# Attention and graph convolution on one core: where the last two items' GpSimd additions stand, and who turns the last pair of heads

## The chip, the cores and the metric

The kernel runs on one core of a Trainium2 chip. The metric is the device time of one execution in microseconds (us). The engines are TensorE (PE in the profile, with PEld for its weight loads), VectorE (DVE), ScalarE (ACT), GpSimd (POOL) and the queues that issue DMA transfers (SP and ACT). Each engine works through its own instructions in program order[...].

## What is computed

There are 32 items; each is a 512x512 matrix `x`, and all share one adjacency matrix. Two layers follow each other, each with a residual and a layer norm:

```python
# layer 0: attention with 8 heads of 64, masked by adj
q, k, v = x @ Wq + bq, x @ Wk + bk, x @ Wv + bv
weights = softmax(q k^T / sqrt(64) + where(adj == 0, -1e9, 0))
x = layernorm(x + weights v)
# layer 1: graph convolution
norm_adj = adj * deg**-0.5 (rows) * deg**-0.5 (columns)
x = layernorm(x + norm_adj @ (x @ weight) + bias)
```

All inputs and outputs are 32-bit floats.

## The kernel before

A 512x512 matrix lies in SBUF as four row blocks of 128 partitions. The heads are handled in pairs `g`, in the order `ORDER = (0, 2, 1, 3)`, so there are 4 pairs for each of the 32 items and `S = 128` steps `k` in one long loop. A step forms the transposed scores of its pair in two halves (`scores`: TensorE into the PSUM tile `sc`, VectorE into the tile `e` with the mask, ScalarE the exponential in place), multiplies the previous pair's `e` with its values (`values`, PSUM tile `av`, heads on the partitions, rows along the free axis), and adds the `e` tiles up on GpSimd (`accumulate`), for the softmax sums that TensorE then forms (`sums`).

The projections use a seven-product scheme on 256-wide halves, and so does the convolution's second product (`second`, seven pieces `s[0]` to `s[6]`). Each piece writes one of three PSUM buffers `mm` and is then added to the outputs by VectorE, or copied aside by ScalarE and added by GpSimd (`extend`) in item 30, whose convolution has `aside` set.

After the pairs of an item comes its finish: `inverse` (TensorE turns the sums, VectorE takes the reciprocal), `add` or, in the last item, `add_pair` (values times reciprocal plus residual, per block of 128 rows and pair), `measure` (mean and variance), `root` (GpSimd raises to the power -0.5), `norm` (the normalized block into `yT`, or `wv` in the last item, and a rounded copy `hi` scaled by the degree), `split` (the rest `lo`, so that hi and lo together keep the precision, and then GpSimd adds the layer's bias row `b1_r` to the block). The convolution's first product (`first`, or `block` in the last item) multiplies hi and lo of each block with the adjacency. `grow` scales the residual, `combine` forms the sums that the seven products need.

The work of one item is laid between the steps of the next by lists of pieces that are written out by hand, and the order in the lists is the order on each engine: a wrapper pins every instruction to program order. This is why nearly all rows of the profile have line L44, the wrapper's; rows are told apart by their tile names. The `shares` lists of the last item's branch (lines 783 to 791) say what runs behind the steps S-3, S-2 and S-1; lines 821 to 849 are the tail after the last step, where there is no further pair to hide work behind.

Names used below: `split(i)` makes `lo` of row block i; `s` is the list `second` of item 30's convolution, `h` and `held` that of item 29; `last` and `end` are the finish of item 31; `pairs[2]` and `pairs[3]` are the `add_pair` of the third and fourth pair in order; `early` and `late` are the two halves of `inverse`; `judge` counts how many sums lie in a safe range; `norm[i]` of odd i runs on VectorE in the last item.

The values of a pair must be turned from heads on partitions to rows on partitions. In `values`, VectorE transposes 32x32 blocks of `av` into the tile `yb`, and four DMA transfers put the blocks where they belong in `YT`; for the last pair two of the four are issued by ScalarE's queue.

Of the kernel before, what the change touches and what calls it, by code (L numbers as in the profile page):

```python
# [9 lines left out]
F32 = mybir.dt.float32  # L10
# [7 lines left out]
P = 128  # L18
H = 8
HD = 64  # L20
# [29 lines left out]
def unshifted(  # L50
# [323 lines left out]
    def values(s):  # L374

        b, g, jj = s
        e = E.pop(s)
        if jj == 0:
            AV[b, g] = ps_av.tile([P, N], F32, name="av")
        av = AV[b, g]  # L380
        for l in range(2):
            j = 2 * jj + l
            for k in range(2):
                tensor.matmul(
                    av[k * HD : (k + 1) * HD, :], V[b][:, j, ts(2 * g + k, HD)], e[l][:, k, :],
                    start=j == 0, stop=j == NT - 1,
                )
        if jj == 0:
            return

        yb = work.tile([P, 4, NT, 32], F32, name="yb", bufs=1)
        vector.transpose(
            yb.rearrange("p l i s -> p i l s"), av.rearrange("p (i r l) -> p i l r", i=NT, l=4)
        )
        if g == ORDER[0]:
            if b < B - 1:
                YT[b] = acts.tile([P, NT, D], F32, name="yT")
            else:  # L400
                YT[b] = wv[:, :NT].rearrange("p k u o -> p k (u o)")
        for q in range(4):
            queue = scalar if q > 1 and (b, g) == blocks[-1] else nc.sync
            queue.dma_start(
                YT[b][:, :, (4 * g + q) * 32 : (4 * g + q + 1) * 32],
                yb[32 * q : 32 * (q + 1)],
            )
# [42 lines left out]
    def finish(b):  # L450


        t = {}

        def inverse(cs):
            sT = SM[b]
            p = ps_mm.tile([P, NT, 2, 2, 32], F32, name="mm")
            for i in range(NT):
                tensor.transpose(p[:, i].rearrange("p a k r -> p (a k r)"), sT[:, ts(i, P)], ident)
            if cs[0] == 0:  # L460
                t["inv"] = small.tile([P, NT, H], F32, name="inv")
# [12 lines left out]
        def add(i):  # L474
            y = YT[b][:, i, :]
            vector.tensor_mul(
                y.rearrange("p (h d) -> p h d", h=H), y.rearrange("p (h d) -> p h d", h=H),
                t["inv"][:, i, :, None].to_broadcast([P, H, HD]),
            )
            gpsimd.tensor_add(y, y, R[b][i])  # L480

        def add_pair(i, g):

            y, r = YT[b][:, i, :], R[b][i]
            for h in (2 * g, 2 * g + 1):
                at = slice(h * HD, (h + 1) * HD)
                vector.scalar_tensor_tensor(
                    y[:, at], y[:, at], t["inv"][:, i, h : h + 1], r[:, at], op0=ALU.mult, op1=ALU.add
                )

        def measure(i):
            if i == 0:
                t["mv"] = small.tile([P, NT, 2], F32, name="mv")
            statistics(YT[b][:, i, :], t["mv"][:, i, :])

        def root(i=0, k=NT):
            rstd, add = roots(t["mv"][:, i : i + k], None)
            for n in range(k):
                t["rstd", i + n], t["add", i + n] = rstd[:, n : n + 1], add[:, n : n + 1]

        def norm(i):
            if i == 0:
                if b < B - 1:
                    HI[b], LO[b] = (acts.tile([P, NT, D], F32R, name=k, bufs=1) for k in ("hi", "lo"))
                    LO[b] = [LO[b][:, k, :] for k in range(NT)]
                else:
                    HI[b] = acts.tile([P, NT, D], F32R, name="hi2", tag="v")
                    lo = [acts.tile([P, 2, D], F32R, name="lo2", tag="kq", bufs=5) for _ in range(2)]
                    LO[b] = [lo[k // 2][:, k % 2, :] for k in range(NT)]
            x1 = YT[b][:, i, :]  # L510
            rstd, add = t["rstd", i], t["add", i]
            if b == B - 1 and i % 2:
                vector.tensor_scalar(x1, x1, rstd, add, op0=ALU.mult, op1=ALU.add)
            else:
                scalar.activation(x1, x1, AF.Identity, bias=add, scale=rstd)

            scalar.activation(HI[b][:, i, :], x1, AF.Copy, scale=dis[:, i : i + 1])

        def split(i):
            x1 = YT[b][:, i, :]  # L520
            vector.scalar_tensor_tensor(
                LO[b][i], x1, dis[:, i : i + 1], HI[b][:, i, :], op0=ALU.mult, op1=ALU.subtract
            )
            gpsimd.tensor_add(x1, x1, b1_r)

        def grow(i):
            x1 = YT[b][:, i, :]
            scalar.activation(x1, x1, AF.Copy, scale=rdeg[:, i : i + 1])

        def block(f):  # L530
            return [(0, f, (i,)) for i in range(NT)]

        return dict(
            early=[(0.6, inverse, ((0,),))], late=[(0.6, inverse, ((1,),))],
            pairs=[[(0, add_pair, (i, g)) for i in range(NT)] for g in ORDER],
            halves=[(0, root, (0, 2)), (0, root, (2, 2))],
            inverse=[(0.6, inverse, ((0, 1),))], add=block(add), measure=block(measure), root=[(0, root, ())],
            judge=[(0, judge, ())], norm=block(norm), split=block(split), grow=block(grow),
        )

    def weave(side, main):
# [8 lines left out]
    def convolve(b):  # L550
# [43 lines left out]
        def second(k, i, j):  # L594
# [15 lines left out]
                vector.tensor_add(of(y, 0, 0), of(y, 0, 0), p)  # L610
            elif k == 2:
                vector.tensor_add(t["e1"], t["e1"], p)
                if not aside:
                    extend(2)
            elif k == 3:
                t["u2"] = work.tile([P, 2, HALF], F32, name="u2", bufs=1)
                vector.tensor_add(t["u2"], t["e1"], p)
                if not aside:
                    extend(3)
            elif aside:  # L620
                t[k, "p"] = work.tile([P, 2, HALF], F32, name="side", tag="e", bufs=6)
                scalar.copy(t[k, "p"], p)
# [42 lines left out]
        def store(n, at):  # L665
# [18 lines left out]
            extend=[(0, extend, (k,)) for k in range(2, 7)],  # L684
# [8 lines left out]
    def run(pieces):  # L693
        for _, f, args in pieces:
            f(*args)
# [40 lines left out]
    run(weave(masks, keys_and_queries(0, 1)))  # L736
    one, two = turns(1)
    run(one)
    shares, rest = [], []
    for k in range(S + 1):  # L740
        b, at = divmod(k, G)
        if at == 1:
# [38 lines left out]
                    shares = cut(side, (8, 8, 8, 4))  # L781
            else:
                f, c, last = last, convolve(b - 1), finish(b)
                s, first, norm, split, pairs = c["second"], c["first"], f["norm"], f["split"], last["pairs"]
                shares = [
                    h[3:4] + f["measure"] + f["root"] + h[6:] + norm + f["judge"],
                    h[4:6] + split + last["early"] + first[:2] + held["measure"][:2] + first[2:3]
                    + held["measure"][2:] + first[3:] + c["parts"] + f["grow"],
                    held["root"] + s[:2] + pairs[0] + pairs[1],
                    [],  # L790
                ]
# [8 lines left out]
        if k:  # L800
# [3 lines left out]
            values((*blocks[k - 1], 1))  # L804
            if k % 2 == 0 and k < S:
                sums(blocks[k - 1][0], (k - 1) % G // 2)
        if k < S:
            accumulate((*blocks[k], 0))
            scores((*blocks[k], 1))
            if b == B - 1:  # L810
# [8 lines left out]
            run(shares.pop(0))  # L819

    end, e = last, convolve(B - 1)
    norm, split, block, pairs, extend = end["norm"], end["split"], e["block"], end["pairs"], c["extend"]
    run(end["late"] + s[2:3] + pairs[2] + held["store"] + s[3:4])
    run(sum((pairs[3][i : i + 1] + end["measure"][i : i + 1] for i in (0, 1)), []) + end["halves"][:1] + s[4:5])
    run(sum((pairs[3][i : i + 1] + end["measure"][i : i + 1] for i in (2, 3)), []) + end["halves"][1:] + s[5:6])
    run(norm[:2] + split[:1] + block[:1] + extend[:2] + norm[2:3])
    run(split[1:2] + block[1:2] + extend[2:4] + norm[3:] + split[2:3] + block[2:3] + split[3:] + block[3:] + end["judge"])

# [302 lines left out]
```

## Time and profile before

| what | value |
|---|---|
| time, median of 3 runs | 2931.66 us (2931.45 to 2931.84) |
| profiled span | 2929.5 us |
| granted TensorE clock, mean | 0.995 |
| TensorE busy | 2874.0 us, 98% |
| VectorE busy | 2081.8 us, 71% |
| GpSimd busy | 1813.3 us, 62% |
| ScalarE busy | 1059.1 us, 36% |
| `lo` in items 0 to 30 | 124 instructions, mean 1269 ns, shortest 735 ns |
| GpSimd's bias addition to a block of `yT` | 124 instructions, mean 1391 ns |
| GpSimd's addition of two `e` tiles | 126 instructions, mean 2356 ns |

A row of a timeline gives the start and the length in us, the engine, the operation, the output and inputs, shapes, how many instructions are merged, and in brackets the idle time of the engine just before and what ended it. Times count from the start of the span. In the page's group list, a busy time and a mean are given for each kind of instruction. A busy engine may still be waiting inside an instruction, so the mean of one and the same operation can differ from place to place; the shortest case tells what it takes by itself.

### The profile page before, as it was taken

The numbers are of one execution on the slowest core, as the hardware profiler recorded it, in microseconds if no ns is written. First come the engines' busy times: TensorE is split into PE (matmuls) and PEld (weight loads), VectorE is DVE, ScalarE is ACT, GpSimd is POOL, SyncE is SP. The second block draws the span as 40 slices with busy tenths as digits, with TensorE's granted clock in tenths as the row PEclk, the third lists the DMA queues.
The fourth block names the chain that finished last, engine by engine and source line by source line (L and its number), as shares of the span: only waits on it lengthen the run. The fifth ranks groups of instructions, "written<-read, shape, count | busy, mean of one in ns | idle before, by whom it ended". The sixth has DMA issues, their size and how long they took to land.

```text
span 2929.5 us, 35536 instructions
## 1 busy us (share of the span) xinstructions
PE 2874.0 (98%) x12966; PEld 1885.9 (64%) x12966; DVE 2081.8 (71%) x2926; ACT 1059.1 (36%) x1343; POOL 1813.3 (62%) x1139
## 2 busy tenths in 40 slices
PE   7999999999999999999999999999999999999997
PEld 5666666666666666666666666666666666666655
DVE  6677766677666777666776667776677766677677
ACT  1233333343333433333433334333333333343343
POOL 2566666656666666666666666666666666656665
PEclk9999999999999999999999999999999999999998
DMA  5111122112221121211122211122211122112211
GB/s 130 33 26 47 47 58 51 38 39 51 54 54 41 39 51 47 57 41 40 47 50 55 55 40 36 49 53 54 44 40 47 47 58 54 40 35 49 54 36 52
DMA packets 383401, 142.42 MB, mean 49 GB/s; under 512 B 280049, under 2 KB 349681, under 8 KB 383217
## 3 DMA queue, kind: packets, MB, share of 16 engines
q1 hardware_dynamic: 380720, 138.35, 19.8%
q10 hardware_dynamic: 2496, 1.70, 0.3%
q8 instruction: 104, 1.70, 0.2%
q14 instruction: 81, 0.66, 0.1%
HBM read 72.88 MB, written 33.55 MB: 36 GB/s over the span
## 4 chain that ended last, share of the span: by engine, by line
PE 74%; DVE 16%; ACT 6%; issue 2%; POOL 1%; DMA 0%; SPq 0%; DVEq 0%; POOLq 0%
PE mm L44 47%; PE sc L44 15%; PE av L44 12%; DVE u L44 3%; ACT yT L44 3%; DVE e L44 3%; DVE st L44 3%; ACT hi L44 2%; DVE lo L44 2%; DVE low L44 2%; POOL rstd L44 1%; ACT e L44 1%; DVE mv L44 1%; DVE kq L44 1%; DVE v L44 1%
## 5 line engine op out<-in xcount | busy, mean ns | idle before, releaser
L44 ACT ACTIVATE e<-e 128x1024 f32<-128x1024 f32 x512 | 540.6, 1057 | 1095.1 <-DVE e L44 1076.3
L44 DVE SCALAR_TENSOR_TENSOR e<-sc,maskT 128x1024 f32<-128x1024 f32 x512 | 600.3, 1213 | 83.1 <-PE sc L44 82.7
L44 POOL TENSOR_TENSOR acc<-acc,e 128x1024 f32<-128x1024 f32 x248 | 597.4, 2409 | 64.2 <-ACT e L44 54.4
L44 POOL TENSOR_TENSOR acc<-e 128x1024 f32<-128x1024 f32 x126 | 296.9, 2356 | 382.5 <-ACT e L44 271.4
L44 PE MATMUL sc<-kq 64*128 64x512 f32 x2048 | 518.9, 620 | 14.5 <-DVE e L44 14.5
L44 PE MATMUL mm<-xT,wk 128*128 128x256 f32 x1792 | 469.8, 385 | 1.0 <-DVE off L44 1.0
L44 PE MATMUL av<-e,v 128*64 128x512 f32 x2048 | 467.9, 599 | 0.0
L44 PE MATMUL mm<-xT,wq 128*128 128x256 f32 x1792 | 459.9, 379 | 0.0
L44 PE MATMUL mm<-wv,xT 128*128 128x256 f32 x1792 | 407.2, 385 | 18.2 <-DVE xT L44 11.7
L44 PEld LDWEIGHTS mm<-xT,wk 128*128 128x128 f32 x1792 | 332.7, 190 | 113.4 <-issue 69.7
L44 PEld LDWEIGHTS mm<-wv,xT 128*128 128x128 f32 x1792 | 338.3, 192 | 93.2 <-issue 24.3
L44 PEld LDWEIGHTS mm<-xT,wq 128*128 128x128 f32 x1792 | 340.9, 190 | 45.6
L44 PEld LDWEIGHTS sc<-kq 64*128 64x128 f32 x2048 | 174.2, 186 | 297.9 <-issue 171.9
L44 PEld LDWEIGHTS av<-e,v 128*64 128x64 f32 x2048 | 135.5, 136 | 316.2 <-issue 315.4
L44 DVE TENSOR_TENSOR kq<-u,mm 128x512 f32<-128x512 f32 x128 | 88.0, 688 | 238.0 <-PE mm L44 237.9
L44 POOL TENSOR_TENSOR yT<-yT,xr 128x512 f32<-128x512 f32 x124 | 193.6, 1590 | 80.5 <-DVE yT L44 80.5
L44 POOL TENSOR_TENSOR rstd<-ve,minus_half 128x4 f32<-128x4 f32 (+1 forms) x66 | 66.2, 1003 | 259.3 <-DVE nmu L44 259.3
L44 PE MATMUL mm<-w,zT 128*128 128x256 f32 x992 | 224.6, 379 | 0.0
L44 POOL TENSOR_TENSOR yT<-yT,b_r 128x512 f32<-128x512 f32 x124 | 171.2, 1391 | 56.4 <-DVE lo L44 56.4
L44 PEld LDWEIGHTS mm<-w,zT 128*128 128x128 f32 x992 | 188.4, 190 | 26.8 <-issue 1.5
L44 PE MATMUL mm<-adjT,hi 128*128 128x512 f32 x496 | 203.7, 411 | 0.0
L44 PE MATMUL mm<-adjT,lo 128*128 128x512 f32 x496 | 198.3, 400 | 5.2 <-DVE lo L44 5.2
(124 smaller groups left out, 3178.6 us busy)
## 6 DMA issues: line engine op xcount, KB each, us to landing
x<-in_x_dram SPq DMA_DIRECT2D x256, 128.0 KB, 2.9
out_dram<-y SPq DMA_DIRECT2D x127, 256.0 KB, 2.1
xr<-in_x_dram SPq DMA_DIRECT2D x124, 256.0 KB, 3.5
yT<-yb SPq DMA_DIRECT2D x496, 64.0 KB, 2.5
wv<-in_L_gnn_Wv_dram ACTq DMA_DIRECT2D x8, 128.0 KB, 4.5
wk<-in_L_gnn_Wk_dram SPq DMA_DIRECT2D x8, 128.0 KB, 4.3
wq<-in_L_gnn_Wq_dram SPq DMA_DIRECT2D x8, 128.0 KB, 4.5
yT<-in_adj_dram SPq DMA_DIRECT2D x1, 1024.0 KB, 6.6
```

Source lines behind the costliest of these rows:

```text
L44: return self.tc.keep_in_program_order(op(*args, **kwargs))
```

## The change

It has two aims. The first is that the last pair's values shall not go through VectorE's block transpose and a DMA: they are copied from PSUM to SBUF by ScalarE and VectorE, half each, TensorE transposes them into a PSUM buffer, and `add_pair` reads the values there. The second is the order on GpSimd in the last two items: its additions are put behind the VectorE operations that they keep from running. `split` becomes two parts, `low` (VectorE) and `lift` (GpSimd). In item 30 one `low` is put ahead of the last-but-one pair's second scores, two more between two pieces of `second`, the fourth behind them, then the four lifts, and only then the two additions of that pair's `e` tiles, which were issued with the scores before. In the tail, `extend(2)` and `extend(3)` go directly behind their products, `extend(4)` ahead of the second root, `extend(5)` behind the first lift, and the lifts behind the `lo` of the next blocks; `s[5]` goes ahead of the first `norm`.

```diff
@@ values @@
+        if (b, g) == blocks[-1]:
+            turned = work.tile([P, N], F32, name="avT", tag="yb", bufs=1)
+            scalar.copy(turned[:, :HALF], av[:, :HALF])
+            vector.tensor_copy(turned[:, HALF:], av[:, HALF:])
+            AV[b, g] = turned
+            return
...
-            queue = scalar if q > 1 and (b, g) == blocks[-1] else nc.sync
-            queue.dma_start(
+            nc.sync.dma_start(
@@ finish @@
+        def turn_values(g):
+
+            t["y"] = ps_mm.tile([P, NT, P], F32, name="mm")
+            for i in range(NT):
+                tensor.transpose(t["y"][:, i], AV[b, g][:, ts(i, P)], ident)
...
+                values = t["y"][:, i, ts(k, HD)] if (b, g) == blocks[-1] else y[:, at]
                 vector.scalar_tensor_tensor(
-                    y[:, at], y[:, at], t["inv"][:, i, h : h + 1], r[:, at], op0=ALU.mult, op1=ALU.add
+                    y[:, at], values, t["inv"][:, i, h : h + 1], r[:, at], op0=ALU.mult, op1=ALU.add
...
         def split(i):
-            x1 = YT[b][:, i, :]
-            vector.scalar_tensor_tensor(
-                LO[b][i], x1, dis[:, i : i + 1], HI[b][:, i, :], op0=ALU.mult, op1=ALU.subtract
-            )
-            gpsimd.tensor_add(x1, x1, b1_r)
+            low(i)
+            lift(i)
@@ second @@
                 vector.tensor_add(t["e1"], t["e1"], p)
-                if not aside:
-                    extend(2)
+                extend(2)
...
                 vector.tensor_add(t["u2"], t["e1"], p)
-                if not aside:
-                    extend(3)
+                extend(3)
@@ the last item's lists @@
+                within = low[:1]
                 shares = [
...
-                    h[4:6] + split + last["early"] + first[:2] + held["measure"][:2] + first[2:3]
-                    + held["measure"][2:] + first[3:] + c["parts"] + f["grow"],
+                    h[4:5] + low[1:3] + h[5:6] + low[3:] + lift + put_off + put_off + last["early"] + first[:2]
+                    + held["measure"][:2] + first[2:3] + held["measure"][2:] + first[3:] + c["parts"] + f["grow"],
@@ the step loop @@
-        if k < S:
+        if k == S - 2:
+            run(within)
+            scores((*blocks[k], 1))
+            pending += [((*blocks[k], jj),) for jj in range(2)]
+        elif k < S:
@@ the tail @@
-    run(end["late"] + s[2:3] + pairs[2] + held["store"] + s[3:4])
-    run(sum((pairs[3][i : i + 1] + end["measure"][i : i + 1] for i in (0, 1)), []) + end["halves"][:1] + s[4:5])
-    run(sum((pairs[3][i : i + 1] + end["measure"][i : i + 1] for i in (2, 3)), []) + end["halves"][1:] + s[5:6])
-    run(norm[:2] + split[:1] + block[:1] + extend[:2] + norm[2:3])
-    run(split[1:2] + block[1:2] + extend[2:4] + norm[3:] + split[2:3] + block[2:3] + split[3:] + block[3:] + end["judge"])
+    run(end["late"][:1] + pairs[2] + end["late"][1:] + s[2:3] + held["store"])
+    run(sum((pairs[3][i : i + 1] + end["measure"][i : i + 1] for i in (0, 1)), []) + end["halves"][:1] + s[3:5])
+    run(sum((pairs[3][i : i + 1] + end["measure"][i : i + 1] for i in (2, 3)), []) + extend[:1] + end["halves"][1:])
+    run(s[5:6] + norm[:2] + low[:1] + block[:1] + low[1:2] + block[1:2] + lift[:1] + extend[1:2] + norm[2:] + low[2:3])
+    run(block[2:3] + low[3:] + lift[1:2] + block[3:] + lift[2:] + end["judge"])
...
-    run(e["unload"] + e["parts"] + s[6:] + end["grow"] + extend[4:] + c["measure"][:2])
+    run(e["unload"] + e["parts"] + s[6:] + end["grow"] + extend[2:] + c["measure"][:2])
```

`late` now holds two entries: the reciprocal of the second half of the sums, and `turn_values` of the last pair. `extend` of item 30 now holds only `extend(4)` to `extend(6)`.

More of the change, by code (lines that the diff above doesn't have):

```diff
@@ L480, in add @@
             gpsimd.tensor_add(y, y, R[b][i])
+        def turn_values(g):
+            t["y"] = ps_mm.tile([P, NT, P], F32, name="mm")
+            for i in range(NT):
+                tensor.transpose(t["y"][:, i], AV[b, g][:, ts(i, P)], ident)
         def add_pair(i, g):
             y, r = YT[b][:, i, :], R[b][i]
-            for h in (2 * g, 2 * g + 1):
+            for k in range(2):
+                h = 2 * g + k
                 at = slice(h * HD, (h + 1) * HD)
+                values = t["y"][:, i, ts(k, HD)] if (b, g) == blocks[-1] else y[:, at]
                 vector.scalar_tensor_tensor(
-                    y[:, at], y[:, at], t["inv"][:, i, h : h + 1], r[:, at], op0=ALU.mult, op1=ALU.add
+                    y[:, at], values, t["inv"][:, i, h : h + 1], r[:, at], op0=ALU.mult, op1=ALU.add
                 )
@@ L517, in norm, with low, lift @@
             scalar.activation(HI[b][:, i, :], x1, AF.Copy, scale=dis[:, i : i + 1])
-        def split(i):
-            x1 = YT[b][:, i, :]
-            vector.scalar_tensor_tensor(
-                LO[b][i], x1, dis[:, i : i + 1], HI[b][:, i, :], op0=ALU.mult, op1=ALU.subtract
-            )
-            gpsimd.tensor_add(x1, x1, b1_r)
+        def low(i):
+            vector.scalar_tensor_tensor(
+                LO[b][i], YT[b][:, i, :], dis[:, i : i + 1], HI[b][:, i, :], op0=ALU.mult, op1=ALU.subtract
+            )
+        def lift(i):
+            gpsimd.tensor_add(YT[b][:, i, :], YT[b][:, i, :], b1_r)
+        def split(i):
+            low(i)
+            lift(i)
         def grow(i):
@@ L533, in finish @@
         return dict(
-            early=[(0.6, inverse, ((0,),))], late=[(0.6, inverse, ((1,),))],
+            early=[(0.6, inverse, ((0,),))], late=[(0.6, inverse, ((1,),)), (0.6, turn_values, (ORDER[-1],))],
             pairs=[[(0, add_pair, (i, g)) for i in range(NT)] for g in ORDER],
@@ L537, in finish @@
             inverse=[(0.6, inverse, ((0, 1),))], add=block(add), measure=block(measure), root=[(0, root, ())],
-            judge=[(0, judge, ())], norm=block(norm), split=block(split), grow=block(grow),
+            judge=[(0, judge, ())], norm=block(norm), split=block(split), low=block(low), lift=block(lift), grow=block(grow),
         )
@@ L683, in convolve @@
             second=[(2.1, second, (k, *args)) for k, args in enumerate(order)],
-            extend=[(0, extend, (k,)) for k in range(2, 7)],
+            extend=[(0, extend, (k,)) for k in range(4, 7)],
             halves=[[(0, measure_half, (n, i)) for n in range(2)] for i in range(2)],
@@ L738, in unshifted @@
     run(one)
-    shares, rest = [], []
+    shares, rest, within = [], [], []
     for k in range(S + 1):
@@ L783, in unshifted @@
                 f, c, last = last, convolve(b - 1), finish(b)
-                s, first, norm, split, pairs = c["second"], c["first"], f["norm"], f["split"], last["pairs"]
+                s, first, low, lift, pairs = c["second"], c["first"], f["low"], f["lift"], last["pairs"]
+                within = low[:1]
                 shares = [
-                    h[3:4] + f["measure"] + f["root"] + h[6:] + norm + f["judge"],
-                    h[4:6] + split + last["early"] + first[:2] + held["measure"][:2] + first[2:3]
-                    + held["measure"][2:] + first[3:] + c["parts"] + f["grow"],
+                    h[3:4] + f["measure"] + f["root"] + h[6:] + f["norm"] + f["judge"],
+                    h[4:5] + low[1:3] + h[5:6] + low[3:] + lift + put_off + put_off + last["early"] + first[:2]
+                    + held["measure"][:2] + first[2:3] + held["measure"][2:] + first[3:] + c["parts"] + f["grow"],
                     held["root"] + s[:2] + pairs[0] + pairs[1],
@@ L821, in unshifted @@
     end, e = last, convolve(B - 1)
-    norm, split, block, pairs, extend = end["norm"], end["split"], e["block"], end["pairs"], c["extend"]
-    run(end["late"] + s[2:3] + pairs[2] + held["store"] + s[3:4])
-    run(sum((pairs[3][i : i + 1] + end["measure"][i : i + 1] for i in (0, 1)), []) + end["halves"][:1] + s[4:5])
-    run(sum((pairs[3][i : i + 1] + end["measure"][i : i + 1] for i in (2, 3)), []) + end["halves"][1:] + s[5:6])
-    run(norm[:2] + split[:1] + block[:1] + extend[:2] + norm[2:3])
-    run(split[1:2] + block[1:2] + extend[2:4] + norm[3:] + split[2:3] + block[2:3] + split[3:] + block[3:] + end["judge"])
+    norm, low, lift, block, pairs, extend = end["norm"], end["low"], end["lift"], e["block"], end["pairs"], c["extend"]
+    run(end["late"][:1] + pairs[2] + end["late"][1:] + s[2:3] + held["store"])
[3 more added lines that the diff above has]
+    run(block[2:3] + low[3:] + lift[1:2] + block[3:] + lift[2:] + end["judge"])
     count = small.tile([P, 1], F32, name="count")
```

## The prediction

> **What bounds the kernel now.** I read the page's shares first. TensorE is busy for 98% of the span, so over 30 of the 32 items an edit on VectorE or GpSimd is worth nothing unless TensorE waits for it. The change touches only the last two items, so I then looked at their last 95 us by stretches (columns: stretch, length, busy time and instructions of PE, PEld, DVE, ACT and POOL, the granted clock, DMA share, GB/s).
>
> ```profile
> PE 2874.0 (98%) x12966; PEld 1885.9 (64%) x12966; DVE 2081.8 (71%) x2926; ACT 1059.1 (36%) x1343; POOL 1813.3 (62%) x1139
> 2834.00:2847.00 13.00, 13.00 (x66) 5.98 (x65) 11.21 (x21) 7.25 (x10) 5.50 (x5) 1.00 0.14 20
> 2847.00:2857.00 10.00, 4.84 (x14) 2.30 (x13) 9.70 (x7) 2.35 (x3) 9.47 (x5) 0.68 0.01 2
> 2857.00:2865.00 8.00, 8.00 (x27) 6.03 (x28) 2.75 (x8) 2.06 (x4) 2.38 (x3) 0.76 0.00 0
> 2865.00:2881.00 16.00, 16.00 (x80) 6.55 (x76) 11.02 (x26) 7.22 (x10) 10.54 (x8) 1.00 0.12 17
> 2892.00:2904.00 12.00, 11.20 (x42) 8.84 (x42) 11.63 (x18) 5.21 (x9) 11.37 (x9) 0.87 0.00 0
> 2904.00:2918.00 14.00, 12.72 (x56) 10.02 (x56) 13.08 (x27) 2.79 (x6) 13.32 (x12) 1.00 0.01 2
> ```
>
> TensorE loses half of the stretch from 2847 to 2857, where VectorE and GpSimd both look full; in the next one it is full but at a clock of 0.76. From 2892 on it is again VectorE and GpSimd that are full together. The timeline of the first hole says why:
>
> ```profile
> 2847.53 2.36 POOL L44 TENSOR_TENSOR wq<-e 128x1024 f32<-128x1024 f32 x1 [7.95 <-ACT e L44]
> 2847.91 8.66 DVE L44 SCALAR_TENSOR_TENSOR lo<-yT,dis,hi 128x512 fp32r<-128x512 f32 x4
> 2849.85 2.81 POOL L44 TENSOR_TENSOR wk<-e 128x1024 f32<-128x1024 f32 x1
> 2850.49 0.66 PE L44 MATMUL mm<-adjT,lo 128*128 128x512 f32 x1 [2.56 <-DVE lo L44]
> 2852.61 6.34 POOL L44 TENSOR_TENSOR yT<-yT,b_r 128x512 f32<-128x512 f32 x4
> 2853.25 0.80 PE L44 MATMUL mm<-adjT,lo 128*128 128x512 f32 x1 [1.67 <-DVE lo L44]
> ```
>
> Four lo subtractions take 8.66 us here, 2.17 each. The operation's own length is that of its shortest case, 735 ns among 124. Each lo waits for one GpSimd addition, and each addition for one lo: they alternate. TensorE waits for every lo. In the chain of waits that ended last the same stretch stands as VectorE's, then nearly everything from 2883.7 to 2907.5 with it:
>
> ```profile
> 2847.99 8.59 DVE lo L44 x4
> 2882.13 1.70 ACTq L44 DMA_DIRECT2D wv<-yb  x2
> 2886.46 0.47 DVE L44 SCALAR_TENSOR_TENSOR wv<-wv,inv,wk 128x64 f32<-128x64 f32 x2
> 2895.73 3.47 DVE L44 SCALAR_TENSOR_TENSOR lo<-wv,dis,hi 128x512 fp32r<-128x512 f32 x2
> 2899.13 1.27 DVE L44 TENSOR_SCALAR low<-inv 128x32 f32<-128x32 f32 x1
> 2900.43 1.22 DVE L44 SCALAR_TENSOR_TENSOR low<-inv,low 128x32 f32<-128x32 f32 x1
> 2904.00 0.68 DVE L44 COPY xT<-sc 128x512 f32<-128x512 f32 x1
> ```
>
> The first line is the chain's, the rest the timeline's. The turned values of the last pair are sent at 2882.1 and first used at 2886.46. The tiny check of the sums (128x32) takes 1.27 and 1.22 us, and TensorE's output waits for it until 2904.0.
>
> **What the Trainium skill says.** "SBUF — State Buffer", section Who interferes with whom: VectorE and GpSimd share a port pair as an exclusive lock; a VectorE instruction with two SBUF inputs, or a copy or tensor_scalar in a two-port mode, and a GpSimd instruction reading SBUF exclude each other for their whole length; a VectorE instruction with one SBUF input does not contend. The trace agrees: lo (two SBUF inputs) 2.17 us against 0.735, the tiny low 1.27 against its mean of 203 ns, while the bn_stats between 2856.7 and 2859.7 keep their 0.66 us beside the additions. "TensorE: Matmul & The Clock Gate", section What's actually happening: an idle window of about 3.4 us halves the clock. The trace agrees: 0.63 us records and 0.43 us start to start until 2860.6, then 0.40 and 0.233. "VectorE: DVE Perf Modes", section The three transpose paths: VectorE turns only 32x32 blocks, TensorE a whole 128x128, into PSUM. The kernel before shows both: a block turn plus DMA for the values, and TensorE turns for the sums.
>
> **Part 1: item 30, the lo subtractions before the additions.** low(0) goes in front of the scores of the last-but-one pair, low(1) and low(2) between the two second products, low(3) behind them; on GpSimd the four lifts (yT plus bias) and then the two additions of e follow. By the timeline hi(0) is ready at 2841.2 and GpSimd idles from 2839.6, so low(0) runs alone, 2843.0 to 2843.7. It pushes the two e operations from 2842.97 to 2843.7; nothing on TensorE reads them before the next pair. They end at 2846.05, y takes 0.65 more, low(1) and low(2) run to 2848.05. lift(0) was done by 2845.0; lift(1) starts as low(2) ends and holds 1.27 us, to 2849.3; low(3) waits for that and ends at 2850.0. TensorE starts this block's products at 2847.46, eight of 0.233 us for the first column, so it reaches lo(3) at 2849.1: a stall of 0.9, which is too short to lower the clock. Then 24 products of 0.233 = 5.6 us: the scores of the last pair start at 2856.0 instead of 2864.59. That is 8.6 us.
>
> Does anything eat it before the end of the pairs? GpSimd: lifts to 2852.5, two additions of 2.36 to 2857.2, four parts of 1.3 to 2862.4 (before: 2869.8), so 7.4 earlier; its next addition then needs 2.36 and the last one waits for an exponential, which comes 8.6 earlier: GpSimd has 1.4 us of slack left there. ScalarE: grow needs the lifts at 2852.5 and starts at 2856.6. The last two e buffers come free at 2854.9, wanted at 2862.7. VectorE's measurements end at 2853.4, its next scores come at 2857.1. So the 8.6 us arrive whole at the last product with the values. From here I keep the times of before, and take 8.6 off at the end.
>
> **Part 2: the last pair turned by TensorE.** Removed: one block turn of 0.71 on VectorE, four DMAs and their flight. Added: two half copies out of PSUM. A copy of 128x256 is not in the trace for either engine; VectorE's 128x256 operations take 0.41 to 0.47, ScalarE's 0.464, so 0.4 to 0.47: 2881.4 to 2881.85. Then four transposes, which for the sums take 0.49 to the next product. The values are in PSUM at 2882.5. But now pairs[2] (eight operations of 0.22, to 2884.0) and the e addition of s[2] (product starts 2882.45, plus 1.93 as before: 2884.4 to 2885.05) come first, so the last pair starts at 2885.0 against 2886.46. Its operations read one input in PSUM instead of SBUF; the cost of that at 64 columns isn't shown, and lies between nothing and 0.05 each by the 128x256 rows; I take 0.02. Each block with its measurement keeps 1.34 to 1.36.
>
> **Part 3: what is moved in the tail.** The u addition (0.68) now stands between blocks 1 and 2 of this row. Sum on VectorE: 2885.0 + 4 x 1.35 + 0.25 + 0.66 = 2891.3 + 0.25 for the second mean, against 2892.3: 0.8 earlier. The first root is ready at 2889.05 (before 2890.5). But ScalarE's norm(0) stands behind the copy of s[5]; s[5] needs a PSUM buffer of three, of which the turned values hold one, and the others come free at about 2888.5 (ScalarE's copy of s[4], VectorE's u). So s[5] starts at 2888.7, its copy ends at 2891.2, and norm(0) is 0.7 later than before.
>
> GpSimd now does extend(3) (2 x 1.27) from 2889.0 and extend(4) to 2892.8, ahead of the second root (0.73 and 0.2). If VectorE and GpSimd alternate as in the first hole, norm(1) ends at 2893.2, root to 2894.0, low(0) 2894.7, low(1) 2895.5, lift(0) 2896.8, norm(3) 2897.2, extend(5) 2898.5, low(2) 2899.1, lift(1) 2900.4, low(3) 2901.1, lift(2) 2902.3, lift(3) 2903.7, with the check squeezed between, and 1.2 us of small counts after it. The xT copies come at 2905.0, not 2904.0: 1.0 later. Afterwards no lift is left to fight VectorE's two part subtractions (2.35 for two at 2905.2, 1.3 alone), which returns up to 1.05, but GpSimd's own parts may take the lock between them. The rest of the tail is the same work. I put the tail at +0.8, bounds -2 to +3.
>
> The other edits (the removed ScalarE DMA issues of 1.7, the lists' order) lie beside idle ScalarE time. Sum: -8.6 + 0.8 = -7.8, less than 0.1 of it for the PSUM reads: 2931.66 - 7.7 = 2924.0 us.
>
> **Rivals.** A, the tail gains too (0.18): if VectorE keeps the lock over two operations in a row, as lo(0) and lo(1) do at 2892.74 (1.63 for two), the xT copies come near 2901.5 instead of 2904: -8.6 - 2.5 = 2920.6. Against it: in both holes alternation is what is seen.
> B, within the noise (0.21): lift(1) slips in between low(1) and low(2), so that low(3) ends at 2851.2 and the gain is 7.4; and the tail's products stay at half clock, 12 more at 0.19 us, with norm(0) late: +3. 2931.66 - 7.4 + 3 = 2927.3. For it: the tail's clock is 0.87 even now.
> C, slower (0.03): GpSimd, whose additions of e now end at 2857.2 instead of 2852.6, becomes the bound and the sums wait for it, so that nothing of the 8.6 arrives; and the tail runs wholly cold, 32 x 0.19 = 6, with +1 from the lock: 2938.7. Against it: GpSimd's slack above, and a trace in which it idles 2.76 us before the last addition.
>
> **How the numbers follow.** The forecast case has 0.58, A 0.18, B 0.21, C 0.03. The forecast and A are faster by over 0.2% (5.9 us, below 2925.8): 0.76; B is within: 0.21; C slower: 0.03. The range leaves out C, most of A's far side and B's: 2920.5 to 2927.5.
>
> **What would show it.** Right: four lo in the item before last of 0.7 to 1.4 us; no TensorE wait over 1 us between 2847 and 2857 and a clock of 1.0 after it; last scores near 2856; the sums' products about 8.6 earlier; first wv operation of the last pair some 3.6 us after the last product with the values, before 5.1; copies to xT about 1 us later after that product than the 22.7 of before. Wrong: a wait of TensorE on a GpSimd addition before the sums, lo still above 2 us, or the last xT copies moved by more than 3 us against that product.

## The result and the profile after

The changed kernel takes 2920.82 us (2920.1 to 2921.3, 4 runs) against 2931.55 of the kernel before on the same chip: 10.7 us less, a ratio of 0.9963 with a 95% interval of 0.9946 to 0.998. The forecast was 7.7 less, 2924.0. The time lies inside the forecast range, 0.3 us above its lower end, and nearer to rival A.

The page's shares and the stretches of the changed kernel (same columns as before):

```profile
PE 2866.3 (98%) x12970; PEld 1879.0 (64%) x12970; DVE 2076.0 (71%) x2926; ACT 1059.4 (36%) x1344; POOL 1813.4 (62%) x1139
...
2847.00:2857.00 10.00, 9.68 (x42) 6.41 (x42) 5.93 (x13) 5.34 (x9) 10.00 (x6) 1.00 0.00 0
2884.00:2896.00 12.00, 11.37 (x50) 8.86 (x49) 11.62 (x18) 6.52 (x12) 9.42 (x7) 1.00 0.00 0
```

The stretch from 2847 to 2857, where TensorE had lost half, is full and at full clock; GpSimd is just as full, but VectorE now has only 5.93 us in it. The later stretch, where TensorE multiplies the last item's blocks, has a clock of 1.00 instead of 0.87 (2892 to 2904 before). The timeline of item 30:

```profile
2842.22 0.73 DVE L44 SCALAR_TENSOR_TENSOR lo<-yT,dis,hi 128x512 fp32r<-128x512 f32 x1
...
2845.73 1.41 DVE L44 SCALAR_TENSOR_TENSOR lo<-yT,dis,hi 128x512 fp32r<-128x512 f32 x2
...
2847.65 1.19 DVE L44 SCALAR_TENSOR_TENSOR lo<-yT,dis,hi 128x512 fp32r<-128x512 f32 x1
...
2846.55 4.69 POOL L44 TENSOR_TENSOR yT<-yT,b_r 128x512 f32<-128x512 f32 x3 [2.25 <-DVE lo L44]
...
2848.90 0.50 PE L44 MATMUL mm<-adjT,lo 128*128 128x512 f32 x1 [0.32 <-DVE lo L44]
...
2854.92 1.99 PE L44 MATMUL sc<-kq 64*128 64x512 f32 x8
...
2869.73 1.94 PE L44 MATMUL av<-e,v 128*64 128x512 f32 x8
```

The last two stood here in the kernel before:

```profile
2864.59 1.99 PE L44 MATMUL sc<-kq 64*128 64x512 f32 x8
...
2879.40 1.94 PE L44 MATMUL av<-e,v 128*64 128x512 f32 x8
```

The four lo need 3.33 us in all (8.66 before). One runs alone, two in a row, and only the last waits for a lift. TensorE's four waits, 5.2 us in all, have become one of 0.32, and the last pair's scores start at 2854.92 instead of 2864.59. Of those 9.67 us, 0.75 are no part of the change: the scores at 2834.25 before stand at 2833.50 here, ahead of everything that was edited. So item 30 gave 8.9 us.

From there to the tail nothing was lost: the last product with the values starts at 2869.73 instead of 2879.40, again 9.67. The tail, from that start to the last normalization (2911.41 here, 2922.55 before), is 41.68 us long instead of 43.15: another 1.5. Rows of it:

```profile
2878.95 1.99 PE L44 MATMUL mm<-w,zT 128*128 128x256 f32 x8 [0.73 <-ACT side L44]
...
2881.52 0.82 ACT L44 ACTIVATE wv<-wv,add,rstd 128x512 f32<-128x512 f32 x1
...
2881.80 1.27 POOL L44 TENSOR_TENSOR y<-y,side 128x512 f32<-128x512 f32 x1
2883.03 0.89 POOL L44 TENSOR_TENSOR rstd<-ve,minus_half 128x2 f32<-128x2 f32 x1
...
2875.41 0.47 DVE L44 SCALAR_TENSOR_TENSOR wv<-mm,inv,wk 128x64 f32<-128x64 f32 x2
...
2881.84 1.50 DVE L44 TENSOR_SCALAR wv<-wv,rstd,add 128x512 f32<-128x512 f32 x1
2883.27 1.63 DVE L44 SCALAR_TENSOR_TENSOR lo<-wv,dis,hi 128x512 fp32r<-128x512 f32 x2
...
2886.27 3.47 DVE L44 SCALAR_TENSOR_TENSOR lo<-wv,dis,hi 128x512 fp32r<-128x512 f32 x2
2889.66 1.27 DVE L44 TENSOR_SCALAR low<-inv 128x32 f32<-128x32 f32 x1
2890.97 1.21 DVE L44 SCALAR_TENSOR_TENSOR low<-inv,low 128x32 f32<-128x32 f32 x1
...
2893.19 0.68 DVE L44 COPY xT<-sc 128x512 f32<-128x512 f32 x1
```

The last pair starts 3.7 us after the last product with the values ends (2871.67), before it was 5.1. Little of this lasts. s[5] waits 0.73 us for a PSUM buffer, until ScalarE's copy of s[4] is done. The u addition now stands between the last pair's blocks, so the second mean is only 0.8 us earlier. Then norm(1) waits for extend(4) and takes 1.50 us where it took 0.54. The two lo groups and the check (the two `low` rows) are as long as before and end 0.2 us later than before, counted from the start of the last product with the values. Yet VectorE's first xT copy comes 23.46 us after that start, and before it was 24.60 (ScalarE makes the other two of the four copies). The gain lies in two tiny additions between the check and the copies. In the kernel before:

```profile
2901.56 2.49 POOL L44 TENSOR_TENSOR y<-y,side 128x512 f32<-128x512 f32 x2
...
2902.19 0.65 DVE L44 TENSOR_TENSOR count<-count,more 128x1 f32<-128x1 f32 x1
...
2903.07 1.00 DVE L44 TENSOR_TENSOR count<-count,more 128x1 f32<-128x1 f32 x1
```

In the changed kernel:

```profile
2892.72 0.16 DVE L44 TENSOR_TENSOR count<-count,more 128x1 f32<-128x1 f32 x1
...
2893.10 0.16 DVE L44 TENSOR_TENSOR count<-count,more 128x1 f32<-128x1 f32 x1
```

Before, each of the two ends 0.02 us after one of GpSimd's two extend additions, so both waited for them. Now these additions are done earlier, GpSimd's last lift ends at 2892.13, and GpSimd is idle while the counts run: 1.3 us less. The pair took 0.65 to 0.67 and 1.00 us in all three profiles with the old tail order (before, and two of the runs below), and 0.16 each in all with the new one. TensorE's clock is not the cause: before, its products of the blocks ended at 2901.2, 2.8 us ahead of VectorE's copy, although they had begun at half clock.

### The profile page after: what moved, and what is told of

Same layout as the page of the kernel before. It is cut to its first block, busy times and chain, and to the rows that moved or that the text cites. A ratio compares the mean times of both kernels' runs of the same rounds, so it can differ in the third digit from the quotient of the medians.

```text
span 2918.3 us, 35535 instructions
## 1 busy us (share of the span) xinstructions
PE 2866.3 (98%) x12970; PEld 1879.0 (64%) x12970; DVE 2076.0 (71%) x2926; ACT 1059.4 (36%) x1344; POOL 1813.4 (62%) x1139
## 4 chain that ended last, share of the span: by engine, by line
PE 74%; DVE 16%; ACT 6%; issue 2%; POOL 1%; DMA 0%; SPq 0%; DVEq 0%; POOLq 0%; ACTq 0%
PE mm L44 47%; PE sc L44 15%; PE av L44 12%; DVE u L44 3%; ACT yT L44 3%; DVE e L44 3%; DVE st L44 3%; ACT hi L44 2%; DVE lo L44 2%; DVE low L44 2%; POOL rstd L44 1%; ACT e L44 1%; DVE mv L44 1%; DVE kq L44 1%; DVE v L44 1%
```

## The experiments

Medians, with the kernel before on the same chip beside each; differences are to that. The intervals reach 2 to 5 us to each side, so differences of 1 or 2 us between two versions are not shown by the times alone; there the traces have to decide. The letters in the expectations name a theory and its rival.

| run | us | before | difference | ratio, 95% interval |
|---|---|---|---|---|
| item 30's order alone | 2922.97 | 2931.82 | -8.9 | 0.9969 (0.9958 to 0.9980) |
| turn and tail alone | 2930.40 | 2931.82 | -1.4 | 0.9995 (0.9987 to 1.0003) |
| turn alone | 2933.09 | 2931.82 | +1.3 | 1.0003 (0.9994 to 1.0011) |
| additions of e first | 2921.85 | 2931.28 | -9.4 | 0.9969 (0.9956 to 0.9981) |
| four lo in a row | 2925.82 | 2931.28 | -5.5 | 0.9981 (0.9973 to 0.9989) |
| check late | 2921.18 | 2931.28 | -10.1 | 0.9966 (0.9954 to 0.9979) |
| check late, u and norm(0) earlier | 2920.43 | 2931.28 | -10.9 | 0.9965 (0.9951 to 0.9978) |
| changed kernel again | 2921.96 | 2932.32 | -10.4 | 0.9964 (0.9951 to 0.9978) |
| check late, gap filled | 2920.08 | 2932.32 | -12.2 | 0.9958 (0.9944 to 0.9972) |
| gap filled alone | 2921.87 | 2932.32 | -10.5 | 0.9965 (0.9951 to 0.9978) |
| check early | 2921.26 | 2932.32 | -11.1 | 0.9964 (0.9950 to 0.9977) |

**Item 30's order alone.** The kernel before, with this of the change (and `split` in its two parts) and no more:

```diff
+                within = low[:1]
...
-                    h[4:6] + split + last["early"] + first[:2] + held["measure"][:2] + first[2:3]
+                    h[4:5] + low[1:3] + h[5:6] + low[3:] + lift + put_off + put_off + last["early"] + first[:2]
...
+        if k == S - 2:
+            run(within)
+            scores((*blocks[k], 1))
+            pending += [((*blocks[k], jj),) for jj in range(2)]
...
```

> The kernel before with item 30's new order alone (the four low ahead of the lifts, the two additions of e behind them); the tail and the last pair's block turn stay. Theory T (the changed kernel's gain is two sums that add: about 8.9 us in item 30, because TensorE no longer waits for lo and stays at full clock, and about 1.5 us in the tail): 2922.6 us, and the last pair's scores some 8.9 us earlier against the first difference of the two traces. Rival V (the turned values carry the gain, item 30's hole would be filled by another wait): 2930 or more.

Measured: 8.9 us less; its wait and its scores, in TensorE's timeline:

```profile
2849.60 0.50 PE L44 MATMUL mm<-adjT,lo 128*128 128x512 f32 x1 [0.32 <-DVE lo L44]
...
2855.63 1.99 PE L44 MATMUL sc<-kq 64*128 64x512 f32 x8
```

Five sixths of the gain are here, and T's number is met; V falls.

**Turn and tail alone.** The changed kernel with that part put back as it was.

> The changed kernel with item 30's order as it was before, so turned values and the tail's new order alone. T: 1.5 us less than before, 2930.0 us; hole of about 6 us on TensorE in item 30 as before. V: 2924 or less.

Measured: 1.4 us less, near T's number, and V falls. TensorE still waits 5.0 us for the lo of item 30. The interval of the ratio takes in 1, so by the times alone this part is not clear of noise. The trace has VectorE's xT copy 23.48 us after the start of the last product with the values and the tail 41.69 us long, the same as in the changed kernel. The two parts add up: 8.9 + 1.4 = 10.3, against 10.7 and 10.4 in the two measurements of the whole.

**Turn alone.** The kernel before with `turn_values` and the new `values` and `add_pair`, the tail's lists unchanged.

> The kernel before with the last pair's values turned on TensorE and nothing else: the lists of the tail keep their order. T: the turn alone brings nothing: the e addition of s[2] comes 0.7 later since the four transposes stand ahead of s[2], pairs[2] and the u addition follow it, so that the last pair starts no sooner than with the DMA: 2931.6 to 2932.4 us. V: it saves the DMA's wait, 1.5 us or more: 2930 or less.

Measured: 1.3 us more, 0.7 above T's range, but not clear of noise. V falls. In the trace, which is of its slowest run, VectorE's xT copy comes 25.34 us after the last product's start, 0.74 later than before. The timeline says why:

```profile
2883.32 0.42 DVE L44 COPY avT<-av 128x256 f32<-128x256 f32 x1 [0.96 <-ACT avT L44]
...
2886.01 0.69 DVE L44 TENSOR_TENSOR e<-e,mm 128x512 f32<-128x512 f32 x1 [2.10 <-PE mm L44]
...
2888.18 0.68 DVE L44 TENSOR_TENSOR u<-e,mm 128x512 f32<-128x512 f32 x1
2888.78 0.47 DVE L44 SCALAR_TENSOR_TENSOR wv<-mm,inv,wk 128x64 f32<-128x64 f32 x2
```

The copy is done at 2883.7, the first use is at 2888.8: VectorE waits 2.10 us for s[2] behind the transposes, and what stands after that in its order, pairs[2] and u, waits with it, though pairs[2] needs nothing of s[2]. So in the old order the turn is of no use. Whether it is of use in the new one isn't shown: what the new order would give with the DMA was not run, and the 1.4 us that it starts the last pair earlier are used up before the lo groups. The tail's 1.4 us are not divided further.

**What GpSimd holds.** A kernel of its own, without the model's computation, run once.

> A kernel of its own that leaves the whole computation out: one kind of VectorE instruction in a row beside one kind of GpSimd instruction in a row, with nothing between them but what they share. Theory L (what GpSimd holds against VectorE is the reading of its operands, so a 128x2 power, 0.7 us long, hardly holds anything): scalar_tensor_tensor with two SBUF inputs at 0.65 us from start to start alone, 1.9 beside 128x512 additions (one by one in turn), under 0.75 beside powers. Rival H (each GpSimd instruction holds for its whole length, as the prediction reckoned the second root): 1.35 us beside powers. Both: bn_stats (one SBUF input) and the form with one input in PSUM stay near 0.65 beside additions; tensor_scalar 0.46 beside powers by L and 1.2 by H.

The timelines of VectorE and GpSimd; each row is one kind in a row, with count and total length (starts at 3.55, 14.04 and 25.56 run alone, the others in pairs):

```profile
3.55 9.41 DVE L44 SCALAR_TENSOR_TENSOR vo<-va,sc,vb 128x512 f32<-128x512 f32 x12 [0.49 <-DMA va<-in_x_dram]
14.04 10.64 POOL L44 TENSOR_TENSOR go<-ga,gb 128x512 f32<-128x512 f32 x8
25.56 6.09 POOL L44 TENSOR_TENSOR powd<-base,expo 128x2 f32<-128x2 f32 x8
32.34 18.23 DVE L44 SCALAR_TENSOR_TENSOR vo<-va,sc,vb 128x512 f32<-128x512 f32 x12
32.65 16.58 POOL L44 TENSOR_TENSOR go<-ga,gb 128x512 f32<-128x512 f32 x10
51.33 12.59 DVE L44 SCALAR_TENSOR_TENSOR vo<-va,sc,vb 128x512 f32<-128x512 f32 x16
51.52 11.38 POOL L44 TENSOR_TENSOR powd<-base,expo 128x2 f32<-128x2 f32 x14
84.88 11.62 DVE L44 BATCH_NORM_STATS2 st<-va 128x6 f32<-128x512 f32 x16
98.01 12.54 DVE L44 SCALAR_TENSOR_TENSOR vo<-pt,sc,vb 128x512 f32<-128x512 f32 x16
98.33 12.03 POOL L44 TENSOR_TENSOR go<-ga,gb 128x512 f32<-128x512 f32 x9
129.37 11.64 DVE L44 TENSOR_SCALAR vo<-va,sc 128x512 f32<-128x512 f32 x20
```

The operation with two SBUF inputs takes 0.784 us alone (9.41 / 12), 0.787 beside powers (12.59 / 16), and 1.52 beside additions (18.23 / 12, with the first and the last, which run clear of them; each of the ten others takes 1.63). So the power, 0.76 us long (6.09 / 8), holds nothing that can be seen. With one input in PSUM the operation takes 0.784 beside additions, and these keep 1.34 against 1.33 alone; bn_stats takes 0.73 beside additions, which also keep 1.33. tensor_scalar takes 0.58 beside powers (11.64 / 20), not H's 1.2. So L stands and H falls, although L's absolute sizes were off: 0.65 was expected for the operation alone, and 1.9 beside additions. And the exclusion is not of whole lengths: 12 x 0.784 + 10 x 1.33 = 22.7 us of work took 18.2.

**Additions of e first.** The changed kernel, item 30's early low kept, but GpSimd's order among its own additions as before:

```diff
         if k == S - 2:
             run(within)
+            accumulate((*blocks[k], 0))
             scores((*blocks[k], 1))
-            pending += [((*blocks[k], jj),) for jj in range(2)]
+            accumulate((*blocks[k], 1))
```

> The changed kernel with the two additions of e in item 30 issued beside their scores again, so ahead of the lifts on GpSimd; the four low stay early. Theory T (what counts is that the low are early, before the first exponential lets GpSimd start): only low(3) meets an addition, of 2.36 us instead of a lift's 1.27, TensorE's stall before its last lo grows from 0.3 to about 1.6 us: 1.2 us over the changed kernel, 9.5 under before: 2922.3 us. Rival O (the order among GpSimd's own additions is the point): 5 us or more over the changed kernel, 2926 or more.

Measured: 9.4 less, T's number, and O falls. Only the last lo is caught, by an addition of e:

```profile
2848.94 2.29 DVE L44 SCALAR_TENSOR_TENSOR lo<-yT,dis,hi 128x512 fp32r<-128x512 f32 x1
...
2851.28 0.50 PE L44 MATMUL mm<-adjT,lo 128*128 128x512 f32 x1 [1.42 <-DVE lo L44]
```

To have VectorE's operations early is what counts. The order of the additions behind them is worth about 1 us by TensorE's wait (1.42 against 0.32), which the times alone don't show.

**Four lo in a row.**

```diff
-                within = low[:1]
...
-                    h[4:5] + low[1:3] + h[5:6] + low[3:] + lift + put_off + put_off + last["early"] + first[:2]
+                    h[4:6] + low + lift + put_off + put_off + last["early"] + first[:2]
```

> The changed kernel with its four low in a row behind both pieces of the second product, followed by lifts and additions as changed. T: two low run in a row, then lifts and low alternate, low(3) ends some 3.4 us later than in the changed kernel: 2924.5 us, 7 under before. Rival O (behind is enough, the interleaving with the two pieces is not needed): within 1 us of the changed kernel, 2922 or less.

Measured: 5.5 less, so 1.5 us worse than T expected, and O falls. The lo group is nearly as T has it: against the changed kernel its last product starts 3.1 us later, where T had 3.4 for the lo. But behind it TensorE runs at half clock:

```profile
2853.30 0.50 PE L44 MATMUL mm<-adjT,lo 128*128 128x512 f32 x1 [0.94 <-DVE lo L44]
...
2853.90 0.63 PE L44 MATMUL mm<-adjT,lo 128*128 128x512 f32 x1
2854.33 0.63 PE L44 MATMUL mm<-adjT,hi 128*128 128x512 f32 x1
...
2857.28 0.39 PE L44 MATMUL mm<-adjT,lo 128*128 128x512 f32 x1
```

From 2853.90 to 2857.28 eight products stand 0.42 us apart instead of 0.233: 1.5 us. TensorE's waits ahead of them are of 0.78, 0.94 and 0.94 us.

**Check late, and with u and norm(0) earlier.**

```diff
-    run(block[2:3] + low[3:] + lift[1:2] + block[3:] + lift[2:] + end["judge"])
+    run(block[2:3] + low[3:] + lift[1:2] + block[3:] + lift[2:])
...
+    run(end["judge"])
     count = small.tile([P, 1], F32, name="count")
...
+    run(e["stores"][:2])
```

> The changed kernel with the check of the sums and its counts taken from between the last low and the xT copies and put behind the last roots, where VectorE waits 1 us for GpSimd. T (VectorE sets the tail and the two small operations that wait for lifts, 1.27 and 1.21 us, lie on its path): xT copies 2 us earlier, the end 1 to 2 us earlier: 10.7 + 1.5 under before, 2919.6 us. Rival: TensorE's seven products set the tail, or the flag's own way to its reader sets the end: no gain, 2921 or more.

The second run has besides `pairs[3][:1] + end["measure"][:1] + s[3:4] + pairs[3][1:2]` in the tail's second list and `norm[:2] + s[5:6]` in the fourth.

> The check late as in the run beside it, and besides s[3] with its u addition ahead of the last pair's second block (so that extend(3) and extend(4) are off GpSimd before norm(1)), and norm(0) ahead of ScalarE's copy of s[5]. T: norm(1) waits 1.04 us for extend(4) in the changed kernel; some 0.7 of it goes and block(0) starts 0.7 earlier: 0.5 to 1 us under the run with the check late alone, 2918.8 us. Rival: low(0) still waits for hi, the copies come no sooner: the same as with the check late alone.

Measured: 10.1 and 10.9 less, so no gain over the changed kernel's 10.4 to 10.7 that can be told from noise. T's 2919.6 and 2918.8 are missed. The second run's median is 0.7 below the first's, as T has it, but their runs overlap, and its xT copies come no sooner (22.92 us after the start of the last product with the values, against 22.84), as the rival has it. The check shrank as expected (0.17 and 0.19 us at the end), but in these two profiles TensorE's blocks set the copies. With the check late alone:

```profile
2884.28 2.08 PE L44 MATMUL sc<-adjT,hi 128*128 128x512 f32 x4 [2.20 <-ACT hi L44]
2886.15 1.76 PE L44 MATMUL sc<-adjT,lo 128*128 128x512 f32 x4
```

It had idled for 2.2 us and started at half clock (2.08 us for four products); the changed kernel's profile, with the same idle time, started at full clock (1.20). That leaves either TensorE's clock or VectorE as the tail's limit, which the next three runs part.

**Gap filled.** To the check late, `s[6]` is moved from behind block(3) into the gap (the run "gap filled alone" has only this):

```diff
-    run(s[5:6] + norm[:2] + low[:1] + block[:1] + low[1:2] + block[1:2] + lift[:1] + extend[1:2] + norm[2:] + low[2:3])
+    run(s[5:6] + norm[:2] + s[6:] + low[:1] + block[:1] + low[1:2] + block[1:2] + lift[:1] + extend[1:2] + norm[2:] + low[2:3])
...
-    run(e["unload"] + e["parts"] + s[6:] + end["grow"] + extend[2:] + c["measure"][:2])
+    run(e["unload"] + e["parts"] + end["grow"] + extend[2:] + c["measure"][:2])
```

> The changed kernel, unaltered, on the chip of the runs beside it: 10 to 11 us under before, 2920.5 to 2921.5.

> The changed kernel with the check late, and with the seventh product of item 30, s[6], moved from behind block(3) to ahead of block(0), where TensorE idles 2.2 us. Theory W (with the check late alone TensorE's blocks set the tail, and in the profile they began at half clock since TensorE had idled before them; filling the gap keeps the clock and takes 1.7 us of TensorE's work off the path): block(0)'s first four products 1.2 us long instead of 2.08, the xT copies 21.5 us after the last product with the values starts (23.5 in the changed kernel, 22.8 with the check late alone), and 1.5 to 2 us under the changed kernel: 2919.0 us. Rival D (VectorE and GpSimd set the tail in any case): within 0.6 us of the changed kernel.

> The changed kernel with s[6] ahead of block(0) and the check where it was. W: the check on VectorE still holds back the xT copies, so nothing or up to 0.5 us under the changed kernel, 2920.5 us. Rival: TensorE alone sets the tail, then 1.5 us or more under it.

Measured: with both, 1.9 us under the changed kernel on the same chip. None of its five runs (2918.87 to 2921.02) is as long as the shortest of the changed kernel's five (2921.07 to 2922.66), but only by 0.05 us, and the intervals in the table are wider than the difference. With the gap filled alone it is 0.1. The timeline with both:

```profile
2882.32 1.89 PE L44 MATMUL mm<-w,parts 128*128 128x256 f32 x8
2884.68 1.19 PE L44 MATMUL sc<-adjT,hi 128*128 128x512 f32 x4 [0.47 <-ACT hi L44]
...
2892.92 1.29 DVE L44 COPY xT<-sc 128x512 f32<-128x512 f32 x2 [1.63 <-ACT xT L44]
```

With the gap filled alone, TensorE is as early but waits for the copies behind the check:

```profile
2895.35 5.01 PE L44 MATMUL mm<-w,xT 128*128 128x256 f32 x22 [1.85 <-DVE xT L44]
```

With both, VectorE's copies come 21.65 us after the last product with the values starts (2871.27), and the tail is 39.96 us long; in the changed kernel beside it these are 23.47 and 41.68, with the gap filled alone 23.46 and 41.66, with the check late alone 22.84 and 41.48. So W stands by these traces: VectorE's check and TensorE's blocks were two limits close to each other, and to move either alone shortened the tail by 0.2 us or less. How much of the 1.7 us is TensorE's clock and how much the work of s[6] that it no longer has behind the blocks was not run apart. The version with both has the lowest median of all.

**Check early.** The same eight small operations directly behind `pairs[2]`.

> The changed kernel with the check of the sums and its counts put directly behind pairs[2], while GpSimd is idle and VectorE waits 0.41 us for s[2]. W: eight small operations of about 1.5 us in all, 1.0 of it on VectorE's path, against 3.5 us off it later, of which 2 can be used: 0.5 to 1 us under the changed kernel, 2920.0 us. Rival: they cost as much as they save: within 0.3 us.

Measured: 0.7 under the changed kernel, inside what W expected, but the two sets of runs overlap (2920.27 to 2923.23), so it isn't shown to be faster. Nor does its profile show it: VectorE's copies come 23.11 us after the last product with the values starts, but the tail is 41.77 us long, no shorter than the changed kernel's, so the rival isn't refuted. The first block ran at half clock (2.03 us).

## Why the prediction was right, and what it mis-sized

The main mechanism is shown: item 30's order was reckoned at 8.6 us and brought 8.9 alone. Its steps held: low(0) alone, low(1) and low(2) in a row, low(3) behind a lift, clock kept, GpSimd's slack enough. TensorE's stall was 0.32 instead of 0.9, because low(3) ended at 2848.8, where low(2), a lift of 1.27 us and low(3) of 0.74, one behind the other, would have ended at 2849.1. The shift arrived whole at the last product with the values.

In the tail, the last pair's start (3.65 us after the last product; measured 3.7), norm(0) behind s[5] (2891.2 by the clock of before; measured 2881.52 + 9.67 = 2891.2) and norm(1) behind extend(4) are as forecast. The term that was mis-sized is the alternation, "root to 2894.0, low(0) 2894.7, low(1) 2895.5" to "lift(3) 2903.7", and with it the tail's +0.8, measured -1.5. The sign that the prediction gave for the tail, xT copies about 1 us later, failed: they came 1.1 earlier. Placed on the clock of before (9.67 added):

| | forecast | measured |
|---|---|---|
| norm(1) ends | 2893.2 | 2893.0 |
| low(1) ends | 2895.5 | 2894.6 |
| low(3) ends | 2901.1 | 2899.4 |
| lift(3) ends | 2903.7 | 2901.8 |
| VectorE's first xT copy | 2905.0 | 2902.9 |

About 0.7 of the 2.1 comes from counting the root's two small operations as holders of the lock for their length, which the kernel on what GpSimd holds refutes. The trace of before already spoke against it, with two lo that take hardly more than twice their own length beside a root:

```profile
2892.39 0.99 POOL L44 TENSOR_TENSOR rstd<-ve,minus_half 128x2 f32<-128x2 f32 x1 [1.91 <-DVE nmu L44]
2892.74 1.63 DVE L44 SCALAR_TENSOR_TENSOR lo<-wv,dis,hi 128x512 fp32r<-128x512 f32 x2
```

Another 0.8 lies between low(1) and low(3), where each hand-over costs less than the two full lengths, as that kernel also shows (18.2 against 22.7). The rest is in three places of about 0.2 each. The counts were reckoned nearly right, 1.2 us where 1.0 was measured and 2.3 stood before. VectorE's part subtractions gave back nothing (2.36 for two, 2.35 before), which the prediction left open. The end gained 0.3 more: before, VectorE waits 0.48 us at 2912.53 for a GpSimd addition, here it doesn't.

Rival A named the right size (2920.6), in part by luck: it put the copies at 2901.5, they came at 2902.9, and the parts that the traces show, 8.9 and 1.5, sum to less than its 11.1. It has only part of the cause: in the kernel on what GpSimd holds, VectorE doesn't keep the lock over GpSimd's waiting additions; a small GpSimd operation simply doesn't take it for long. B's slip of lift(1) did not happen; its half clock in the tail came with the check late and with the check early, but not in the two profiles of the changed kernel. C fell with item 30's order alone. The Trainium skill, "SBUF — State Buffer", section Who interferes with whom, has the blocking for the whole instruction where it speaks of VectorE's two-port modes; of two SBUF inputs it says that they contend with a GpSimd instruction that reads SBUF. The prediction took the whole length for both. For the 128x512 additions the traces agree that they contend, though not for whole lengths; for the 128x2 power, which reads SBUF too, the measurement (0.787 against 0.784) decides against it.

## What to carry to other kernels

Where two engines exclude each other, put the operations that somebody waits for ahead of the first moment at which the other engine can start, and between operations that read PSUM, rather than in a row: in a row behind, 5 of the 9 us stayed lost here, 1.5 of them by TensorE's clock. Reckon the exclusion by both sides. A small GpSimd operation held up nothing that could be seen (0.787 us against 0.784), but a small VectorE operation waits for a large GpSimd addition (a count took 1.00 us instead of 0.16), so look for small operations on the path too. Ask of each operation that is moved what follows it: here the last pair's earlier start was used up before the lo groups, and the tail's gain came from two tiny additions behind them. A tail with two limits close to each other, here a check on VectorE and TensorE's blocks, gave nearly nothing in the traces until both were moved.

## What was not expected of the hardware

The prediction took a stall of 0.9 us as too short to lower TensorE's clock, and read the first hole as agreeing with an idle window of about 3.4 us. The runs don't show that as a rule. Three waits of 0.78, 0.94 and 0.94 us within 5 us were followed by eight products at half clock (four lo in a row). The longest wait in the first hole of before is 2.56 us, and the products behind it ran at half clock; behind the same wait of 2.56 us in the turn alone the first products ran at full clock (records of 0.50 and 0.39 us instead of 0.66 and 0.63). An idle stretch of 2.20 us lowered the clock in one profile and not in another of nearly the same program. The Trainium skill, "TensorE: Matmul & The Clock Gate", section What's actually happening, has the window running free of the program, which would fit that the same wait goes either way; its idle window of about 3.4 us does not foretell the half clock after three waits of less than 1 us. What decides there stays open.

The two profiles of the changed kernel differ by 2.3 us, and not by such chance in the tail, which is 41.68 us long in both: 1.6 us stand already after the first 255 us of the span, and 0.7 come behind the last normalization.
